# Keeping three windows of the intermediate image in SBUF between two layers, and moving their stores

## The chip, the cores and the metric

The kernel runs on one core of a Trainium2 chip. The metric is the device time of one execution in microseconds (us), the median of several runs; lower is better. TensorE is called PE (its weight loads PEld), VectorE DVE, ScalarE ACT, GpSimd POOL and SyncE SP; SP, ACT and POOL also issue DMAs.

## The reference

Two residual layers on an image x of 48 channels and 256 x 256 pixels, in float32. `_gn` is a group norm over 16 groups of 3 channels.

```python
# layer 0: x = x + L0(gn(x))
qkv = dwconv3x3(einsum('bchw,oc->bohw', x, w_qkv), w_dw)
q, k, v = split(qkv, 3)                 # each cut into 4x4 patches, 8 heads of 96 values
q = l2norm(q); k = l2norm(k)
attn = softmax(einsum('bhcn,bhcm->bhnm', q, k) * temperature)
out = fold(einsum('bhcn,bhnm->bhcm', v, attn))
out = einsum('bchw,oc->bohw', out, w_proj)
# layer 1: x = x + L1(gn(x)), on windows of 64 x 64 pixels
out = einsum('bcphqw,twW,thH,tcC->bCpHqW', xb, Ws, Hs, Cs)      # t runs over 3
```

## The kernel before

Layer 0 begins with the group norm's statistics and the projection to q, k and v, whose results go to DRAM. The attention then runs head by head (`for h in range(NH)`, 8 heads) and in each head over 16 groups of two query blocks. In one group PE computes the scores of two blocks (`logits`, L344), ACT takes their exponential (L563), DVE the reciprocal of the sums and the scaled values vn (L576 to L582), and PE the weighted sums in four parts k (`weigh`, L592), which DVE adds up in `oacc` (L603). All engines stand in the order in which this part is written (`tc.manual_schedule()`). When a head ends, `store(h, m)` for m = 0 to 7 transposes the sums (L609), copies them (ACT, L611, two buffers `oo`) and writes them to the DRAM buffer `os_` through POOL's DMA queue (L613), two DMAs for each m.

The pools of the attention are then closed and the output projection begins, L727 to L755. It has eight tiles t. Tile t holds 16 image rows of the upper half of the image on partitions 0 to 47, and the 16 rows that stand 128 below them on partitions 48 to 95. Of each tile SP loads the attention's result `pot` (from `os_`) and x (`pxt`), 1.5 MB each as two DMAs; PE multiplies by the block matrix `wp`, four times two matmuls of 512 columns (L739); DVE adds the result to x in place, in four additions (L746), and gathers the statistics of the sum in eight `bn_stats` (L750); POOL's queue stores the sum, which is x1, in DRAM as `x1s` (L755). Here the order of each engine's instructions is set by a scheduler, which knows the engines' work and not the other traffic.

The projection's PSUM tiles take the place of the attention's, so that the first L739 waits until ACT's last L611 has read the last transposes.

After the last tile `group_stats` (L135 to L153) makes mean and reciprocal deviation of each group, and a second small matmul (L763) makes the deviation again in the layout of two halves on partitions 0 and 64 (`rstd2`). The matrices Cs are scaled by it (`csn`, L775), and a bias comes from the mean (L779, L781).

Layer 1 works in eight units u: four windows of 64 rows, two halves of 128 columns. Each has three contractions: `over_c` over the channels (PE L834, with x1 as the stationary operand; DVE L841 subtracts the bias into `lzt`), `over_w` (PE L856, ACT copies, L863) and `over_h` (PE L873). `residual` adds the rows of x1 (DVE L885) and sends them out on POOL's queue (L888). Before its use x1 is loaded twice from `x1s`, with different layouts: by channels (`load_x`, L808, three buffers, two units ahead) and by rows (`load_rows`, L817, two buffers for a whole unit). The first `over_c` stands alone; each later one is interleaved with the unit before. In this part too all engines keep the written order. Three lines of it:

```python
parts[u, q].append(over_w(u, c0, c0 + 4))   # for b in 0, 1, each followed by two steps of over_c(u + 1)
over_h(*late)                               # after both b: the third before
late = u, q
```

Of the kernel before, what the change touches and what calls it, by code (L numbers as in the profile page):

```python
# [16 lines left out]
C = 48  # L17
# [3 lines left out]
KS = 4  # L21
# [23 lines left out]
def conv_preact_kernel(  # L45
# [47 lines left out]
    wp = const.tile([P2, P2], F32, name="wp")  # L93
    nc.vector.memset(wp, 0.0)
    for s in range(2):
        r = slice(s * C, (s + 1) * C)
        for h in range(NH if s == 0 else H0):
            o = s * M0 + h * HC if h < H0 else (h - H0) * HC
            nc.scalar.dma_start(
                out=(wq[r] if h < H0 else wr[0:C])[:, o : o + HC].rearrange("c (z e) -> c z e", z=3),  # L100
                in_=w_qkvT.rearrange("c (z h e) -> h c z e", z=3, h=NH)[h],
            )
        nc.scalar.dma_start(out=wp[r, r], in_=w_projT)
# [22 lines left out]
    mean1 = const.tile([P2, 1], F32, name="mean1")  # L126
    rstd1 = const.tile([P2, 1], F32, name="rstd1")
# [7 lines left out]
    def group_stats(st, mean, rstd, pool, pspool):  # L135

        mv = pool.tile([P2, 2], F32, name="mv")
        nc.vector.bn_aggr(mv, st.rearrange("p n s -> p (n s)"))
        pm = pspool.tile([P2, 1], F32, name="pm", tag="pstat")
        nc.tensor.matmul(pm, lhsT=gm, rhs=mv[:, 0:1], start=True, stop=True)  # L140
        nc.vector.tensor_copy(mean, pm)
        d = pool.tile([P2, 1], F32, name="gsd")
        nc.vector.tensor_sub(d, mv[:, 0:1], mean)
        e = pool.tile([P2, 1], F32, name="gse")
        nc.vector.scalar_tensor_tensor(e, d, d, mv[:, 1:2], ALU.mult, ALU.add)
        pv = pspool.tile([P2, 1], F32, name="pv", tag="pstat")
        nc.tensor.matmul(pv, lhsT=gm, rhs=e, start=True, stop=True)
        f = pool.tile([P2, 1], F32, name="gsf")
        nc.vector.tensor_scalar_add(f, pv, EPS)
        g = pool.tile([P2, 1], F32, name="gsg")  # L150
        nc.scalar.activation(g, f, AF.Sqrt)
        nc.vector.reciprocal(rstd, g)
        return mv, e  # L153
# [255 lines left out]
    with tc.tile_pool(name="xn", bufs=1) as xnp, tc.tile_pool(name="cst", bufs=1) as cst, tc.tile_pool(  # L409
# [19 lines left out]
        group_stats(st0, mean0, rstd0, cst, nps)  # L429
# [48 lines left out]
    cv = attention.enter_context(tc.tile_pool(name="cv", bufs=1))  # L478
# [42 lines left out]
    with tc.tile_pool(name="ahead", bufs=2) as ah, tc.tile_pool(name="ae", bufs=3) as ae, tc.tile_pool(  # L521
# [94 lines left out]

        load_query(0, 0)
# [14 lines left out]
        with tc.manual_schedule():  # L632
            load_query(0, 1)
            block = scores(0, 0)
            for h in range(NH):
                more = h + 1 < NH
                rows = {r: Depthwise(h + 1, r) for r in range(CR + 1)} if more else {}
                for g in range(NG):
                    p, d, n = rows.get(g - 2), rows.get(g - 1), rows.get(g)

                    if h == 0 and 0 < g <= 6:
# [40 lines left out]
                    for k in range(NK):  # L682
# [28 lines left out]
                        if g == NG - 1 and k > 0:  # L711
                            for m in range(2 * k - 2, 2 * k):
                                store(h, m)
            for m in range(6, 8):
# [5 lines left out]
    RP = TP // PX * KS  # L720
    NP = TP
    with tc.tile_pool(name="pj", bufs=3) as pj, tc.tile_pool(name="pjs", bufs=1) as pjs, tc.tile_pool(
        name="pps", bufs=3, space=PSUM
    ) as pps, tc.tile_pool(name="pp1", bufs=1, space=PSUM) as pp1:
        st1 = pjs.tile([P2, HALF * W // 512, 6], F32, name="st1")
        ov = os_.rearrange("t (c k) n -> t c k n", k=KK)
        for t in range(HALF // RP):  # L727
            ot = pj.tile([P2, KK, NP], F32, name="pot")
            xt = pj.tile([P2, RP, W], F32, name="pxt")
            for s in range(2):  # L730
                r = slice(s * C, (s + 1) * C)
                y0 = s * HALF + t * RP
                nc.sync.dma_start(out=ot[r], in_=ov[s * (NT // 2 // TP) + t])
                nc.sync.dma_start(out=xt[r], in_=xc[:, y0 : y0 + RP, :])
            xv = xt.rearrange("p (py ki) (px kj) -> p ki kj py px", ki=KS, kj=KS)
            for ki in range(KS):
                ps = pps.tile([P2, KS, NP], F32, name="pps")
                for i in range(0, KS, 2):
                    nc.tensor.matmul(  # L739
                        ps[:, i : i + 2, :],  # L740
                        lhsT=wp,
                        rhs=ot[:, ki * KS + i : ki * KS + i + 2, :],
                        start=True,
                        stop=True,
                    )
                nc.vector.tensor_add(  # L746
                    xv[:, ki], ps.rearrange("p k (py px) -> p k py px", py=RP // KS), xv[:, ki]
                )
            for i in range(0, RP, 2):
                nc.vector.bn_stats(  # L750
                    st1[:, (t * RP + i) // 2, :], xt[:, i : i + 2, :].rearrange("p a b -> p (a b)")
                )
            for s in range(2):
                y0 = s * HALF + t * RP
                nc.gpsimd.dma_start(out=x1s[:, y0 : y0 + RP, :], in_=xt[s * C : (s + 1) * C])  # L755

        gm2 = pjs.tile([P2, 64 + C], F32, name="gm2")
        nc.vector.memset(gm2, 0.0)
        for o in (0, 64):
            nc.vector.tensor_copy(gm2[:, o : o + C], gm[:, 0:C])  # L760
        mv1, e1 = group_stats(st1, mean1, rstd1, pjs, pp1)
        pc1 = pp1.tile([64 + C, 1], F32, name="pc1", tag="pstat")
        nc.tensor.matmul(pc1, lhsT=gm2, rhs=e1, start=True, stop=True)  # L763
        rstd2 = l1c.tile([64 + C, 1], F32, name="rstd2")
        nc.vector.tensor_scalar_add(rstd2, pc1, EPS)
        nc.scalar.activation(rstd2, rstd2, AF.Sqrt)
        nc.vector.reciprocal(rstd2, rstd2)

        csn = l1c.tile([64 + C, T3 * C], F32, name="csn")
        for s in range(2):  # L770
# [4 lines left out]
            nc.vector.tensor_scalar_mul(csn[r], csn[r], rstd2[r])  # L775
# [5 lines left out]
        nc.vector.tensor_copy(cbias, pb1)  # L781


    with tc.tile_pool(name="lx", bufs=3) as lx, tc.tile_pool(name="lz", bufs=2) as lz, tc.tile_pool(
        name="lr", bufs=2
    ) as lr, tc.tile_pool(name="ly", bufs=4) as ly, tc.tile_pool(name="ps1", bufs=2, space=PSUM) as ps1, tc.tile_pool(
# [171 lines left out]
```

## Time and profile before

| | us |
|---|---|
| median of 3 runs | 3771.0 (3754.03 to 3777.11) |
| the profiled execution | 3774.41 |
| its span | 3772.6 |
| last attention matmul (L592) starts its last piece | 3298.4 |
| first projection matmul (L739) | 3318.2 |
| end of the last bn_stats (L750) | 3455.9 |
| csn ready (L775) | 3461.6 |
| layer 1's matmuls run without a stop from | 3475.2 |

PE is busy for 93% of the span, DVE for 58%, ACT for 45%, POOL for 16%; the mean granted clock of PE is 0.97. The times are on the clock of the profiled execution, which starts with its first instruction. A group in a listing has the line, engine and operation, the tiles written and read, partitions x elements, the number of instructions, busy time and mean, and what ended the idle time before it. In a listing by time the columns are the start, the time and the instruction, with the idle time before it in brackets. DMA transfers show in the queues' shares and as what ends a wait.

### The profile page before, as it was taken

To read this page: it belongs to the slowest core of one execution; us is meant where nothing else is said; L and a number is where in the kernel's file an instruction comes from. 1 tells how busy PE (TensorE), PEld (TensorE's weight loads), DVE (VectorE), ACT (ScalarE), POOL (GpSimd) and SP (SyncE) were. 2 spreads that over 40 slices of the span, in tenths; PEclk is the share of its full clock that TensorE was granted. 3 is DMA by queue.
4 is the path that set the end of the run, shared out by engine and by line. 5 is a ranking of instruction groups with operands and counts; after the bars stand their busy time and mean duration, and the time that the engine had idled before them with its cause. 6 is when DMAs were issued, how large, how long until landed. Compare 5 with 4: busy or idle time off the path is not lost.

```text
span 3772.6 us, 100069 instructions
## 1 busy us (share of the span) xinstructions
PE 3521.1 (93%) x44252; PEld 2916.8 (77%) x44252; DVE 2185.9 (58%) x3514; ACT 1715.5 (45%) x2667; POOL 597.5 (16%) x593
## 2 busy tenths in 40 slices
PE   1877999999999999999999999999999999955998
PEld 0335777788888888888888888888888888812776
DVE  5463675169727962896299439934992222256664
ACT  0224565555545554555455445545554444300222
POOL 0031121012301220122122112211221100010011
PEclk9988999999999999999999999999999999966999
DMA  6575666534433542354245424542543100199784
GB/s 144 170 172 159 178 192 177 166 111 118 114 83 99 126 113 73 104 125 107 84 106 122 101 77 113 119 104 75 125 114 93 46 19 23 31 242 199 128 145 91
DMA packets 307826, 441.64 MB, mean 117 GB/s; under 512 B 98474, under 2 KB 232954, under 8 KB 303160
## 3 DMA queue, kind: packets, MB, share of 16 engines
q1 hardware_dynamic: 253668, 269.65, 27.7%
q0 software_dynamic: 48320, 156.61, 18.5%
q10 hardware_dynamic: 5396, 8.88, 1.1%
q8 instruction: 351, 5.75, 0.7%
q14 instruction: 91, 0.75, 0.1%
HBM read 234.76 MB, written 199.95 MB: 115 GB/s over the span
## 4 chain that ended last, share of the span: by engine, by line
PE 84%; DMA 5%; issue 2%; ACT 0%; SPq 0%; DVE 0%; POOL 0%; ACTq 0%; POOLq 0%
PE big L344 37%; PE big L592 36%; PE pb L856 4%; PE pa L834 2%; PE pc L873 2%; PE big L185 2%; DMA x1s<-pxt 1%; DMA pxt<-in_x_dram 1%; DMA t<-ot 1%; PE pt L609 1%; PE pst L546 1%; PE pn L258 1%; DMA kt<-qkv 0%; DMA os__70<-oo 0%; DMA lxq<-x1s 0%
## 5 line engine op out<-in xcount | busy, mean ns | idle before, releaser
L563 ACT ACTIVATE e<-big,nmx 128x1024 f32<-128x1024 f32 x1024 | 1143.9, 1118 | 833.8 <-PE big L344 622.4
L344 PE MATMUL big<-kt,qt 128*128 128x512 f32 x6144 | 1438.9, 393 | 44.4 <-DMA qt<-qkv 31.6
L592 PEld LDWEIGHTS big<-vn,e 128*64 128x64 f32 x32768 | 1365.8, 137 | 83.4 <-ACT e L563 45.1
L592 PE MATMUL big<-vn,e 128*64 128x96 f32 x32768 | 1423.5, 247 | 5.0 <-ACT ot L188 3.1
L344 PEld LDWEIGHTS big<-kt,qt 128*128 128x128 f32 x6144 | 1145.1, 188 | 307.6 <-issue 46.2
L603 DVE TENSOR_TENSOR oacc<-big,oacc 128x768 f32<-128x768 f32 x480 | 458.1, 954 | 708.5 <-PE big L592 708.5
L239 DVE SCALAR_TENSOR_TENSOR acc<-pad,dwt,acc 126x1024 f32<-126x1024 f32 x592 | 766.2, 1295 | 39.1 <-ACT acc L220 23.5
L297 POOL TENSOR_TENSOR ol<-o,oh 126x1024 fp32r<-126x1024 f32 x78 | 187.1, 2399 | 925.3 <-DVE ss L254 800.9
L576 DVE TENSOR_REDUCE zt<-zs 128x1 f32<-128x4 f32 x256 | 38.9, 152 | 360.4 <-ACT e L563 360.4
L563 ACT ACTIVATION_READ_ACCUMULATOR e<-big,nmx 128x1 f32 x1024 | 196.2, 192 | 0.0
L841 DVE TENSOR_TENSOR lzt<-pa,cbias 128x864 f32<-128x864 f32 (+1 forms) x88 | 137.0, 1628 | 96.9 <-PE pa L834 96.9
L863 ACT COPY lyt<-pb 128x512 f32<-128x512 f32 x144 | 84.5, 586 | 212.9 <-PE pb L856 212.9
L302 POOL DMA_DIRECT2D qkv<-o x72 | 88.6, 1230 | 517.6 <-DVE zu L578 248.9
L613 POOL DMA_DIRECT2D os__70<-oo x128 | 65.2, 515 | 599.6 <-ACT oo L611 598.9
L250 ACT ACTIVATE sq<-acc 126x1024 f32<-126x1024 f32 x74 | 78.2, 1057 | 156.3 <-issue 111.1
L284 DVE TENSOR_TENSOR o<-acc,y 126x1024 f32<-126x1024 f32 x74 | 147.6, 1995 | 0.0
L856 PEld LDWEIGHTS pb<-wsb,lzt 128*64 128x64 f32 x2304 | 125.8, 138 | 27.6 <-issue 19.5
L856 PE MATMUL pb<-wsb,lzt 128*64 128x128 f32 x2304 | 141.7, 279 | 1.3 <-issue 1.3
L188 ACT ACTIVATE ot<-big,bias 108x1024 f32<-108x1024 f32 x64 | 71.1, 1112 | 153.7 <-PE big L185 81.4
L739 PE MATMUL pps<-pot,wp 96*96 96x512 f32 x128 | 78.2, 779 | 58.9 <-DMA pot<-os__70 58.9
L220 ACT ACTIVATE acc<-pad,dwt 126x1024 f32<-126x1024 f32 x74 | 84.1, 1137 | 83.0 <-DMA pad<-t 83.0
L318 POOL DMA_DIRECT2D kt<-qkv x44 | 22.9, 527 | 575.8 <-PE big L344 554.5
(116 smaller groups left out, 1904.5 us busy)
## 6 DMA issues: line engine op xcount, KB each, us to landing
pad<-t SPq DMA_DIRECT2D x78, 761.9 KB
qkv<-ol POOLq DMA_DIRECT2D x78, 504.0 KB, 8.9
qkv<-o POOLq DMA_DIRECT2D x72, 504.0 KB, 6.9
qkv<-oh POOLq DMA_DIRECT2D x70, 504.0 KB, 7.4
t<-ot SPq DMA_DIRECT2D x128, 217.7 KB
qt<-qkv SPq DMA_DIRECT2D x176, 96.0 KB
xs<-in_x_dram SPq DMA_DIRECT2D x128, 96.0 KB
os__70<-oo POOLq DMA_DIRECT2D x128, 96.0 KB, 2.1
```

Source lines behind the costliest of these rows:

```text
L220: nc.scalar.mul(self.acc, self.pad[:, 0:KS, 0:W], dwt[:, self.h, 0:1])
L239: nc.vector.scalar_tensor_tensor(self.acc, self.pad[:, dy : dy + KS, dx : dx + W], dwt[:, self.h, tap : tap + 1], self.acc, ALU.mult, ALU.add,
L284: nc.vector.tensor_tensor(self.o.rearrange("p (a b) x -> p a b x", a=KS), self.acc.rearrange("p a (x b) -> p a b x", b=KS), self.y.rearran ...
L297: eng.tensor_sub(self.ol, self.o, self.oh.bitcast(F32))
L302: eng.dma_start(out=qkv[self.h][i].rearrange("j (c k) n -> (j c) k n", k=KK)[:, :, px], in_=self.o if i == 2 else (self.ol if i else self. ...
L344: nc.tensor.matmul(ps[:, i, :], lhsT=qt[:, r, q0 : q0 + 128], rhs=kts[2 * j + i][:, r // 2, :], start=(r == 0), stop=(r == 2),)
L563: nc.scalar.activation(e[:, j * 1024 : (j + 1) * 1024], ps.rearrange("p a b -> p (a b)"), AF.Exp, bias=nmx[:, b : b + 1], accum_out=zs[:, ...
L592: nc.tensor.matmul(ps[p : p + 64, j // 4, j % 4 * HD : (j % 4 + 1) * HD], lhsT=e[:, mb * 128 + p : mb * 128 + p + 64], rhs=vn, start=(i == 0),
L603: nc.vector.tensor_add(oaccs[h, k], ps[:, :, : 4 * HD], oaccs[h, k])
L841: nc.vector.tensor_tensor(zv[:, :, y0 : y0 + n, :], pa[:, :, : n * T3 * C].rearrange("p s (y k) -> p s y k", y=n), cbias.rearrange("p (u v ...
L856: nc.tensor.matmul(pb[s * WS : (s + 1) * WS, i, :], lhsT=zts[u][:, t * C + c + i, :], rhs=wsb[:, t, :], start=True, stop=True,)
L863: nc.scalar.copy(yt[:, t, :], pb.rearrange("p i x -> p (i x)"))
```

## The change

Tiles of x1 stay in SBUF for three of the four windows, and layer 1's channel contraction reads them there. In parts:

1. The projection's tile t is now half t mod 2 of window t // 2: 16 rows of the window's upper 32 rows on partitions 0 to 47, and 16 rows of its lower 32 rows on partitions 64 to 111. These are the layout and the place from which `over_c` reads. `wp` has its two copies at partitions 0 and 64, and each of the old matmuls becomes two, on PE's tile at row and column 0 and on that at row and column 64 (the first has 64 output columns, of which 16 are zero).
2. The partitions 48 to 63 of each window's x tile have to be zero: a memset of partitions 32 to 63 over 8192 elements stands before the loads of x into each, on DVE for window 0 and on POOL for windows 1, 2 and 3.
3. `convolution` is a new pool of its own for the depthwise convolution, so that its memory can be freed before the last head. In the first group of the last head (h = 7, g = 0) the tile of window 0 is zeroed on DVE and loaded by four DMAs on SP. In the last group, after k = 1, the first `pot` (here `pa`) is loaded.
4. SP's instructions in the projection stand in the written order. Window 1's x1 is stored by POOL's queue as before; those of windows 0, 2 and 3 are stored by SP after all loads. 
5. `group_stats` takes its matrix as an argument and works on 112 partitions, so that the second deviation (`pc1`, `rstd2`) is not needed. The matrix `gm2` is loaded by four DMAs instead of two copies on DVE.
6. Layer 1 takes the windows in the order 0, 2, 3, 1. There is no `load_x`. Window 1's x1 is loaded from `x1s` once, in the buffer of window 0, at the start of unit 1. The rows are loaded in thirds of a unit, with three buffers of a third. `over_h` of the third before stands between the two `over_w` of a third, and `lyt` has three buffers instead of four.

```diff
+                    if not more and g == 0:
+                        convolution.close()
+                        xw = ctx.enter_context(tc.tile_pool(name="xw", bufs=1, side="right"))
...
+                        xts[0] = xw.tile([64 + C, 2 * RP, W], F32, name="xwt")
+                        nc.vector.memset(xts[0][32:64], 0.0)
+                        for sub in range(2):
+                            load_input(xts[0], 0, sub)
...
+                        if not more and g == NG - 1 and k == 1:
+                            pots[0] = pa.tile([64 + C, KK, TP], F32, name="pa")
+                            load_output(pots[0], 0)
...
+        NTP = HALF // RP
+        with tc.manual_schedule(engines={mybir.EngineType.SP}):
+            for t in range(NTP):
+                w, sub = divmod(t, 2)
+                if t:
+                    pots[t] = pj.tile([64 + C, KK, TP], F32, name="pot")
+                    load_output(pots[t], t)
+                if w:
+                    if sub == 0:
+                        xts[w] = (pjs if w == 1 else xk).tile([64 + C, 2 * RP, W], F32, name="xk")
+                        nc.gpsimd.memset(xts[w][32:64], 0.0)
+                    load_input(xts[w], w, sub)
...
+                    ps = pps.tile([128, KS, TP], F32, name="pps")
+                    for i in range(0, KS, 2):
+                        for s in range(2):
+                            m = 64 if s == 0 else C
+                            nc.tensor.matmul(
+                                ps[s * 64 : s * 64 + m, i : i + 2, :],
+                                lhsT=wp[s * 64 : s * 64 + C, 0:m],
+                                rhs=pots[t][s * 64 : s * 64 + C, ki * KS + i : ki * KS + i + 2, :],
...
+                if w == 1:
+                    store_x1(w, sub, nc.gpsimd)
+
+            for w in (0, 2, 3):
+                for sub in range(2):
+                    store_x1(w, sub, nc.sync)
+        group_stats(st1, gm2, mean1, rstd1, pjs, pp1)
...
-        units = [(yw, xh) for yw in range(H // WS) for xh in range(2)]
+        units = [(yw, xh) for yw in (0, 2, 3, 1) for xh in range(2)]
...
-            xq = xqs[u]
+            xq = xts[yw]
...
-            for u in range(2):
-                load_x(u)
...
+                if u == 1:
+                    xts[1] = xw.tile([64 + C, HW, W], F32, name="xwt")
+                    for s in range(2):
+                        nc.sync.dma_start(
+                            out=xts[1][s * 64 : s * 64 + C], in_=x1s[:, WS + s * HW : WS + (s + 1) * HW, :]
+                        )
...
                 for q in range(NQ):
+                    load_rows(u, q)
...
-                    if late:
-                        over_h(*late)
+                        if b == 0 and late:
+                            over_h(*late)
```

## The prediction

> **What bounds the kernel now.** The page gives a span of 3772.6 us, the attention to about 3300. I read the busy time by stretches first:
>
> ```profile
> 3340.00:3360.00 20.00, 10.88 (x21) 3.80 (x20) 13.58 (x13) 0.00 (x0) 1.03 (x2) 0.74 1.03 307
> 3400.00:3420.00 20.00, 8.89 (x16) 3.12 (x16) 16.79 (x20) 0.00 (x0) 2.06 (x4) 0.69 1.02 268
> 3456.00:3475.00 19.00, 3.16 (x10) 2.24 (x10) 4.23 (x13) 0.41 (x2) 0.00 (x0) 0.50 0.94 141
> 3495.00:3765.00 270.00, 267.61 (x3776) 202.73 (x3776) 149.40 (x102) 84.45 (x144) 32.05 (x46) 0.99 0.68 120
> ```
>
> After the stretch and its length come PE, PEld, DVE, ACT, POOL, then PE's clock, DMA share and GB/s. The projection has its DMA engines full (1.02) with PE and DVE waiting; from 3495 layer 1 is all PE. The queues in the projection (3335 to 3435), then in the kernel's opening stretch of loads alone (30 to 68): packets, MB, share of 16 engines.
>
> ```profile
> q1 hardware_dynamic: 1451, 17.88, 73.1%
> q0 software_dynamic: 768, 9.44, 27.4%
> ...
> q1 hardware_dynamic: 370, 4.15, 51.9%
> q10 hardware_dynamic: 369, 3.92, 47.4%
> ```
>
> A unit is one tile's load or store, 1.573 MB. In the projection a load takes 73.1 x 1.573 / 17.88 = 6.43 us and a store 27.4 x 1.573 / 9.44 = 4.57: 17.4 a tile, the period seen. Loads alone take 37.7 x 1.573 / 8.07 = 7.35. In order of time, the seams:
>
> ```profile
> 3288.29 5.34 PE L592 MATMUL big<-vn,e 128*64 128x96 f32 x124 [1.87 <-DVE vn L582]
> 3295.11 1.52 POOL L613 DMA_DIRECT2D os__70<-oo  x3 [325.57 <-ACT oo L611]
> 3301.78 2.03 POOL L613 DMA_DIRECT2D os__70<-oo  x4 [4.20 <-ACT oo L611]
> 3317.59 1.02 POOL L613 DMA_DIRECT2D os__70<-oo  x2 [3.02 <-ACT oo L611]
> 3318.17 9.01 PE L739 MATMUL pps<-pot,wp 96*96 96x512 f32 x16 [6.52 <-DMA pot<-os__70]
> 3407.66 7.65 DVE L746 TENSOR_TENSOR pxt<-pps,pxt 96x1024 f32<-96x1024 f32 x4 [3.21 <-DMA pxt<-in_x_dram]
> 3451.02 4.85 DVE L750 BATCH_NORM_STATS2 st<-pxt 96x6 f32<-96x512 f32 x8
> 3461.01 0.61 DVE L775 TENSOR_SCALAR csn<-csn,rstd 48x144 f32<-48x144 f32 x2
> 3475.19 3.21 PE L834 MATMUL pa<-csn,lxq 48*128 48x144 f32 x22 [5.19 <-DMA lxq<-x1s]
> ```
>
> The last head's stores hop through ACT, POOL and a DMA until 3318; eight tiles follow, with 7.65 + 4.85 = 12.5 us of DVE each inside 17.4; statistics end at 3461.6, and layer 1 waits until 3475.2 for the stores and the reload. Two groups price the memsets:
>
> ```profile
> L413 POOL MEMSET zr<- 128x258 f32 x1 | 0.3, 318 | 0.0
> masks.py:197 POOL MEMSET ident<- 128x128 f32 x1 | 0.2, 205 | 0.3 <-POOLq L947 0.3
> ```
>
> (318 - 205) / 130 = 0.87 ns per element of a partition.
>
> **What the Trainium skill says.** DMA: Bandwidth & Descriptors, section on queues, rings and completion order: an engine goes round the queue rows it has work for, packet by packet. The trace agrees: the small L613 stores land in 2.1 us at the median of 128, but in 5.1 to 6.7 us here, beside loads. TensorEngine Tiling (Array Packing), section Tiling Modes: different tiles can run LdWeights and Matmul in parallel. L873 agrees: 24 records of 64x64 tiles in 2.73 us of the chain, 0.114 each, where L739's of the same 512 columns follow every 0.43. TensorE: Matmul & The Clock Gate, Part 1: default is half clock, released by activity. L739's weight loads come every 0.85 us at the start of a burst and every 0.43 after 4 to 7 us.
>
> **The change part by part**, on the old trace's clock.
>
> 1. Last head, first group. DVE zeroes 8192 elements a partition: row L453 (1134 elements, 1003 ns) and L790 (384, 378) give 0.83 ns, 6.9 us, from 2928.0 to 2934.9, before the two normalisations; the weights are first wanted at 2938.2, so those cover it with some 2 us. SP then issues 3.1 MB of x ahead of the query loads for two blocks on: 14.7 us of DMA from 2936.5, query data after that until about 2955 to 2959 with the stores of that time, wanted at 2957.8 (L344). Cost 0 to 4, I take 1.
>
> 2. The memsets on POOL. In the built order those for windows 2 and 3 stand before the last head's stores, and wait for the last vn (3288.24). 2 x 8192 x 0.87 + 2 x 0.1 = 14.5 us (no row is this long; bounds 12 and 18, which move PE's start by as much): stores begin at 3302.9, not 3295.1. The old hops took 22.2 us to ACT's last copy, which the first L739 waits for (PSUM). Four pairs of stores hop one behind the other, since there are two oo buffers. Without neighbours a hop is 0.6 (copy) + 0.3 + 1.0 (two issues) + 2.1 (landing), about 4 us, in all 13.6: PE at 3317. With loads beside every hop it stays at 22.2: 3326. The first hop now finds the DMA queues empty, the later ones meet the early load of pot 0 and those of pots 1 and 2, so I take 20.3 and PE at 3323.5. Early loading gains nothing there: another wait comes last.
>
> 3. Window 1's memset waits for those stores to land (3329) and takes 7.2: its x load, and every load behind it on SP, issues at 3336.5 (3330 to 3338). Tile 2 wants it only at about 3353, as pots 1, 2 and window 0 are there.
>
> 4. The tiles. DVE: first add 5 us after PE's start (3.9 before; the order starts three PSUM tiles before finishing one), then 8 x 12.6 (12.5 and small gaps): 3429. DMA: from 3336.5, 11 load units and 2 store units, at 11 x 6.43 + 2 x 4.57 = 80 or 11 x 7.35 + 2 x 4.57 = 90; if a store adds only what it added to two lone loads before, 17.4 - 14.7 = 2.7, the upper one is 86. I take 83, then 2 to land and 12.5 of DVE on the last tile: 3434 (3425 to 3446). Stores of windows 0, 2, 3 (12 DMAs) stand on SP after all loads. PE has 32 records a tile, in pairs: 6.8 us warm, 13.7 cold, and a burst warms in 4 to 7; covered by DVE, costing at most a us or so.
>
> 5. Statistics. One pair of tiny matmuls with its sum and root goes (-0.75). ACT's table load (1.28 in the trace, at 3317 under the wait) now stands after the wait for the variance: +1.28. From last bn_stats to csn was 5.75, becomes 6.3; with pb 6.9. x1 is in SBUF: L834 starts at 3441, not 3475.2. Of the 12 stores five wait on SP for ACT's Ws/Hs loads (same semaphores), about 3447, then 2.5 units, 16 us; the first row loads follow, landing near 3468, wanted 43 us after the start (L885 at 3518), 3484. Covered by 16.
>
> 6. Layer 1. PE's work is the same: 297.4 us from 3475.2 to the end. The L808 loads go; PE never waited for them after the first. Row loads come in thirds, three buffers: free 8 us before their third begins, wanted 20 after it. Window 1's reload, 14.7 + rows 2.6 + 2, meets a need 19.5 us later; two PSUM buffers cover a small miss. L873 one step earlier in each third: the last no longer waits for DVE's 1.24: -1.3. Sum 296.1 (bounds 294 and 300).
>
> Sum: 3441 + 296.1 + 1 = 3738.1, 34.5 below the span of 3772.6. The profiled execution took 3774.4, 3.4 above the median 3771.0; 3771.0 - 34.5 = 3736.5, say 3737.
>
> **The rivals.**
> - Loads keep the mixed pace (5.8 a unit) and the hops run free: PE at 3317, DVE-bound, 5 + 101: 3423; that is 11 before the forecast's 3434: 3737 - 11 = 3726. For it: the 307 GB/s of the first stretch above. Against: the opening loads at 213 with full engines. 0.20, range 3718 to 3731.
> - A new wait takes the room: the two halves do not pair on PE (13.7 warm a tile, 109 in all), or loads at 7.35 with late rows. Tiles ending at 3447 (13 late) and 4 to 5 of stalls in layer 1: 3754, up to 3770. 0.11.
> - Slower: PE neither pairs nor warms, 32 x 0.853 = 27.3 a tile, 218 for eight; 3323.5 + 218 + 7 for the last add and bn_stats is 3549, 115 behind the forecast: about 3852. For it: PEclk of 0.66 to 0.74 here, and PE waits every tile. Against: L873's packing; a PE so busy has no idle to cool in. Slower by 1% means a span of 3810, so tiles that end at 3810 - 296.1 - 1 - 6.9 = 3506: it decides from (3506 - 3328) / 8 = 22 us a tile. 0.05.
>
> **How the numbers follow.** Forecast 0.64, own range 3729 to 3752. About 1% (37.7 us) is what a measurement here tells from no change: 3733.3. A quarter of the forecast's chance, 0.16, lies below it, with the first rival 0.36 faster; 0.48 + 0.11 = 0.59 within; 0.05 slower. Leaving out 0.05 of the first rival, most of the second and the third, the range is 3724 to 3754.
>
> **What would show it.** POOL memsets of 7.2 us from 3288, twice; PE's first projection matmul near 3323; tile starts 12.5 to 15 apart; a table load between variance and root; L834 (L872 then) starting 7 us after the last bn_stats; 296 from there. Wrong, if POOL's memsets are of another size, tiles take 17 again, or PE shows row waits in layer 1.

## The result, and the profile after

The changed kernel takes 3804.5 us (median of 4 runs, 3797.9 to 3810.3), the kernel before 3771.8 beside it: 1.0086 times the time, with a 95% interval of 1.0064 to 1.0109. So it is slower by 0.9%, where 34 us less were forecast; 3804 lies far above the range of 3724 to 3754. The profiled execution after took 3797.9, with a span of 3796.1.

The two traces by stages, in us, with the forecast on the same marks. Each stage ends where the next begins. "First product of layer 1" is, in the kernel before, the one from which its products run without a stop.

| stage | before | forecast | after |
|---|---|---|---|
| to the end of the last vn (L582, L584 after) | 3288.2 | 3289.2 | 3300.1 |
| to the issue of window 1's first x load | | 48.3 | 61.1 |
| to the end of the last bn_stats | 167.6 from vn | 97.5 | 115.3 |
| to the first product of layer 1 (L834, L872) | 19.3 | 7.0 | 6.7 |
| layer 1 to the end | 297.4 | 296.1 | 312.9 |
| span | 3772.6 | 3738.1 | 3796.1 |

(The forecast's rows come from its 3336.5, 3434 and 3441, with the one us of its step 1 in the first row.) The forecast is 58.0 us short: 10.9 in the last head, 12.8 in the hops, 17.8 with the tiles, 16.8 in layer 1, and -0.3 in the statistics. Only the last-named came out as forecast; the four others are longer. Of the 58.0, 34.5 are the gain that was forecast and did not come, and 23.5 are what the span is longer than before.

Last head, PE in order of time (start, time, instruction; in brackets the idle time before it and what ended it):

```profile
2965.48 2.61 PE L594 MATMUL big<-vn,e 128*64 128x96 f32 x57
2971.93 6.93 PE L594 MATMUL big<-vn,e 128*64 128x96 f32 x128 [3.84 <-issue]
2984.45 0.90 PE L594 MATMUL big<-vn,e 128*64 128x96 f32 x7 [5.59 <-issue]
2985.28 5.00 PE L344 MATMUL big<-kt,qt 128*128 128x512 f32 x14
```

PE stands twice in the middle of a group of equal matmuls, and no semaphore is named: "issue" means that the profile shows nothing that it waited for. The kernel before has no wait of PE at all between 2940 and 3000. PE is also slower after the first stall: 128 matmuls in 6.93 us, where the same number took 5.50 at 2936.7; its clock is 0.83 between 2970 and 2980, and 1.00 before 2970.

The seams behind it, on POOL, ACT and PE:

```profile
3300.19 13.79 POOL L784 MEMSET xk<- 32x8192 f32 x2 [332.10 <-DVE vn L584]
3313.93 2.02 POOL L615 DMA_DIRECT2D os__70<-oo  x4
3351.48 1.01 POOL L615 DMA_DIRECT2D os__70<-oo  x2 [3.80 <-ACT oo L613]
3354.24 6.92 POOL L784 MEMSET xk<- 32x8192 f32 x1 [1.74 <-DMA os__70<-oo]
```

```profile
3335.64 0.58 ACT L613 COPY oo<-pt 96x512 f32<-96x512 f32 x1 [12.57 <-DMA os__70<-oo]
3343.61 0.58 ACT L613 COPY oo<-pt 96x512 f32<-96x512 f32 x1 [7.39 <-DMA os__70<-oo]
```

```profile
3351.29 10.87 PE L793 MATMUL pps<-pa,wp 48*64 48x512 f32 x32 [5.95 <-issue]
```

The two memsets take 13.8 us (14.5 forecast), and the stores begin 13.9 us after the last vn. But from the first pair of stores to the last it takes 37.6 us, since ACT's copy waits up to 12.6 for an old store to land. PE's first product of the projection starts 0.1 us after the end of ACT's last copy (3351.19), which it waits for; "issue" only says that the profile names no releaser.

The tiles on DVE, the DMA queues in two stretches (3365 to 3390, then 3425 to 3450: packets, MB, share of 16 engines), and the busy times of the same two (stretch, length, PE, PEld, DVE, ACT, POOL, PE's clock, DMA share, GB/s):

```profile
3417.25 5.71 DVE L800 TENSOR_TENSOR xk<-pps,xk 112x1024 f32<-112x1024 f32 x3 [5.98 <-DMA xk<-in_x_dram]
3434.24 5.77 DVE L800 TENSOR_TENSOR xk<-pps,xk 112x1024 f32<-112x1024 f32 x3 [4.53 <-DMA xk<-in_x_dram]
```

```profile
q1 hardware_dynamic: 317, 3.88, 102.5%
...
q1 hardware_dynamic: 461, 5.69, 101.0%
```

```profile
3365.00:3390.00 25.00, 21.64 (x62) 6.96 (x62) 23.38 (x23) 0.00 (x0) 0.00 (x0) 0.73 1.02 155
3425.00:3450.00 25.00, 25.00 (x51) 7.64 (x50) 19.22 (x22) 0.00 (x0) 0.00 (x0) 0.51 1.01 227
```

The DMA engines are full, as before, but move 155 GB/s where the kernel before moved 251 to 307. A load unit of 1.573 MB, alone on the queues, takes 1.025 x 25 x 1.573 / 3.88 = 10.4 us in the first stretch and 7.0 in the second. DVE takes 12.5 us a tile, and 14.3 in the two early tiles in which it also waits for PE (up to 1.3 at a time). In tiles 4 and 5, counted from 0, it waits for x: their first additions start 20.3 and 17.0 us after those of the tile before. In the last tile it takes 15.0 us, 2.2 of them waits for PE.

Statistics and layer 1 (ACT and PE in order of time, then PE's waits from 3480 on: us in total, times, longest):

```profile
3480.80 1.28 ACT L152 ACT_TABLE_LOAD   x1 [129.61 <-DVE gsf L151]
```

```profile
3483.20 0.60 PE L872 MATMUL pa<-csn,xwt 48*128 48x144 f32 x1
...
3553.39 2.08 PE L872 MATMUL pa<-csn,xk 48*128 48x144 f32 x14 [3.88 <-issue]
3555.39 4.39 PE L894 MATMUL pb<-wsb,lzt 128*64 128x128 f32 x48
```

```profile
PE pb L894 <- DVE lzt L879: 9.2, 7, 1.3
PE pa L872 <- issue: 3.9, 1, 3.9
```

The statistics went as forecast. In layer 1 PE now waits seven times for DVE's `lzt`, and stands once more with the label "issue", while window 1 is loaded back; the 48 products after it take 4.39 us instead of 2.86 to 2.93.

### The profile page after: what moved, and what is told of

The parts are those of the page before. It is cut to its first block, busy times and chain, and to the rows that moved or that the text cites. A ratio compares the mean times of both kernels' runs of the same rounds, so it can differ in the third digit from the quotient of the medians.

```text
span 3796.1 us, 100386 instructions
## 1 busy us (share of the span) xinstructions
PE 3555.5 (94%) x44378; PEld 2926.7 (77%) x44378; DVE 2192.9 (58%) x3511; ACT 1716.4 (45%) x2666; POOL 611.1 (16%) x584
## 5 line engine op out<-in xcount | busy, mean ns | idle before, releaser
L894 PEld LDWEIGHTS pb<-wsb,lzt 128*64 128x64 f32 x2304 | 127.4, 139 | 38.1 <-issue 31.2
L894 PE MATMUL pb<-wsb,lzt 128*64 128x128 f32 x2304 | 143.1, 281 | 10.6 <-DVE lzt L879 9.2
L254 DVE TENSOR_REDUCE ss<-sq 126x64 f32<-126x1024 f32 x80 | 97.5, 1220 | 23.2 <-ACT sq L250 23.2
```

What stands on the lines that cost most here:

```text
L254: nc.vector.tensor_reduce(self.ss, self.sq.rearrange("p a (x b) -> p x a b", b=KS), AX.XY, ALU.add)
L894: nc.tensor.matmul(pb[s * WS : (s + 1) * WS, i, :], lhsT=zts[u][:, t * C + c + i, :], rhs=wsb[:, t, :], start=True, stop=True,)
```

## The experiments

Each kernel is the changed one with the edit shown, unless it says otherwise; `...` stands for lines left out. What is read is a stage of its trace; the totals of single runs differ for reasons outside the stage (the kernel before took 3766 to 3789 in 28 runs beside one group of these). "The tiles" are the time from the first projection matmul to the last bn_stats. In four kernels whose tile code is equal (the changed one, loads spread, loads behind, layer 1 mended) they took 125.2, 130.7, 128.9 and 131.8 us, so that single runs do not tell apart what differs by less than some 7 us there.

### Last head: spread the loads

```diff
-                        for sub in range(2):
-                            load_input(xts[0], 0, sub)
+                    if not more and 1 <= g <= 4:
+                        sub, s = divmod(g - 1, 2)
+                        nc.sync.dma_start(
+                            out=xts[0][s * 64 : s * 64 + C, sub * RP : (sub + 1) * RP], in_=xc[:, image_rows(0, s, sub), :]
+                        )
```

> The changed kernel, with window 0's four input loads (0.79 MB each) issued one per group at the top of groups 1 to 4 of the last head instead of all four at the top of group 0; the DVE memset stays where it is. Theory A (TensorE's instruction refills stand behind the 3.1 MB backlog of the loads, which made the two stalls of 3.8 and 5.6 us labelled issue): at most three packets per DMA engine stand ahead of a refill, the two stalls fall under 1 us, and the last normalisation of V ends 10 to 13 us earlier than in the changed kernel (near 3288 instead of 3300.1 us on its trace); everything behind keeps its length. Theory C (the memset on DVE, or the new order of the last head, costs the time): the last normalisation stays near 3300.

Measured: from the first exponential of the head to the last vn 354.0 us. It is 354.0 before and 367.3 after. PE has no wait between 2940 and 3000. The memset on DVE is still there, so it costs nothing; the 13.3 us come from the loads' being issued in one piece. The run took 3791.5 us.

### Last head: the block of loads behind the query loads

```diff
-                        for sub in range(2):
-                            load_input(xts[0], 0, sub)
...
                     elif more:
                         load_query(h + 1, g + 2 - NG)
+                    if not more and g == 0:
+                        for sub in range(2):
+                            load_input(xts[0], 0, sub)
```

> The changed kernel, with the four input loads of window 0 issued behind the query loads of the same group on SP, still in one piece. Theory A (instruction refills behind the backlog): the backlog is the same 3.1 MB, so TensorE still stands 7 to 10 us with the label issue in the groups behind it, and the last normalisation of V stays within 3 us of 3300. Theory B (the query loads, queued behind the input loads on SP, come late for the scores): the stalls go, and it ends near 3288 to 3290.

Measured: 361.7 us for the head, last vn at 3298.6, and one stall instead of two:

```profile
2983.53 0.90 PE L594 MATMUL big<-vn,e 128*64 128x96 f32 x7 [6.11 <-issue]
```

So the order on SP is not the cause of 7.7 of the 13.3 us; at most 5.6 belong to it, or to the fact that one packet fewer of the following kind fell into the backlog. What PE waited for shows in the packet records of a queue that the profile calls "instruction" (q8, 16 KB each, called refills here; start, and duration in brackets, us):

```
kernel          refills on q8 between 2940 and 2990                                PE goes on at
before          2941.32  2948.31  2961.71  2969.67  2974.61  2988.91               no stall
after           2946.30  2968.86 (1.63)  2981.63 (1.43)  2985.62                    2971.93, 2984.45
loads behind    2943.83  2951.00  2965.52  2980.41 (1.68)  2989.84                  2983.53
loads spread    2942.43  2948.75  2964.68  2972.30  2975.92                         no stall
```

In each of the three stalls PE goes on 1.4 us after such a packet ends. That these packets carry PE's instructions is read from the counts: from one of them to the next PE runs 128 matmuls at the median (127 in the kernel before), with about as many weight loads; the kernel before has 351 packets for 44,252 matmuls. Up to the late packets PE had run 254 matmuls since the last one in the changed kernel, and 257 with the loads behind, that is two packets' worth, and then it stood; after the first late packet it ran 128 more and stood again. In the changed kernel the two packets start at 2968.86 and 2981.63, and the 3.1 MB of x, issued from 2959.5, have all passed the DMA engines at 2982.2. So the refills of PE's instructions came late while the loads filled the DMA engines; that they stood in line there is the reading that fits both edits.

### Hops: the memsets behind the stores

```diff
-        with tc.manual_schedule(engines={mybir.EngineType.SP}):
+        with tc.manual_schedule(engines={mybir.EngineType.SP, mybir.EngineType.Pool}):
+            for w in (1, 2, 3):
+                xts[w] = (pjs if w == 1 else xk).tile([64 + C, 2 * RP, W], F32, name="xk")
+                nc.gpsimd.memset(xts[w][32:64], 0.0)
             for t in range(NTP):
...
-                    if sub == 0:
-                        xts[w] = (pjs if w == 1 else xk).tile([64 + C, 2 * RP, W], F32, name="xk")
-                        nc.gpsimd.memset(xts[w][32:64], 0.0)
```

> The changed kernel, with the memsets of windows 1, 2 and 3 on POOL put in program order behind the last head's stores, instead of those of windows 2 and 3 ahead of them. If the 13.8 us of the two memsets stand on the path in full: the first store is issued within 1 us of the last normalisation of V's copy chain, the time from the end of the last normalisation to the first projection matmul falls from 51.2 to about 37 us, and the end comes 11 to 14 us earlier (near 3783 on its own span). Rival: the slow landings of the stores (5 to 13 us each beside the loads of the attention output) alone set the chain, the early start only waits longer at the next landing, and it stays above 47 us.

Measured: from the last vn to the first projection matmul 46.2 us instead of 51.2, and the run took 3801.6 us. Neither expectation gave that size. The first store is issued 8.5 us after the last vn, but from the first to the last it is still 37.9 (ACT in order of time):

```profile
3305.80 0.58 ACT L613 COPY oo<-pt 96x512 f32<-96x512 f32 x1 [0.45 <-DMA os__70<-oo]
3322.93 0.58 ACT L613 COPY oo<-pt 96x512 f32<-96x512 f32 x1 [16.56 <-DMA os__70<-oo]
```

The rival's mechanism, the slow landings, is the one that shows. And the 5 us were lost again with the tiles: 139.2 us, 125.2 in the changed kernel.

### Hops: no load beside the stores

With the edit above, and in the loop of the tiles (pot 0 is no longer loaded in the last head, and window 1's input, issued ahead of all pots, waits for the memset behind the stores):

```diff
+            for sub in range(2):
+                load_input(xts[1], 1, sub)
             for t in range(NTP):
-                if t:
-                    pots[t] = pj.tile([64 + C, KK, TP], F32, name="pot")
-                    load_output(pots[t], t)
+                pots[t] = (pj if t else pa).tile([64 + C, KK, TP], F32, name="pot" if t else "pa")
+                load_output(pots[t], t)
...
```

> The changed kernel, with no large load beside the last head's stores: the three memsets of windows 1 to 3 stand on POOL behind the stores, window 1's input loads wait for the first of them, and all loads of the attention output (the one issued in the last head too) stand behind these on SP. Theory (each 2 or 4 KB packet of a store waits for a 16 KB load packet of 1.4 to 1.8 us that its DMA engine runs first): with the queue clear the stores land within 3 us, as the run of small stores in the earlier heads did in 2.1 us, and the time from the first store issued to the last falls from 37.4 us (34 to 38 with or without the memsets ahead) to 17 to 21 us. Rival (the two buffers of oo and the chain of transposes, copies and stores cost that by themselves): it stays above 30 us. The tiles start later, since their loads do: no gain in the end is expected from either.

Measured: 12.3 us from the first store to the last, less than expected (POOL in order of time):

```profile
3309.63 1.52 POOL L615 DMA_DIRECT2D os__70<-oo  x3 [336.67 <-ACT oo L613]
3313.49 2.03 POOL L615 DMA_DIRECT2D os__70<-oo  x4 [1.38 <-ACT oo L613]
3320.86 2.16 POOL L615 DMA_DIRECT2D os__70<-oo  x4 [1.56 <-ACT oo L613]
```

So 25 of the 37.6 us come from the loads beside the stores (with the memsets moved alone it was 37.9). The stores' own packets are short in the records: 0.08 us at the median for 2 KB and 0.23 for 4 KB here, 0.14 and 0.32 beside the loads of the changed kernel. A load packet of 16 KB takes 1.5 us at the median there. That each store packet waits for a load packet is not seen in the records one by one; it is the reading that fits, and it agrees with what the Trainium skill says in DMA: Bandwidth & Descriptors, section on queues, rings and completion order: an engine goes round its rows packet by packet. The kernel before had 2.59 MB of loads between 3295 and 3318 (22.5 us of hops), the changed one 4.72 between 3314 and 3352, since its tiles 0, 1 and 2 read what the first four pairs of stores wrote, where before the lower half of tile 0 waited for the fifth. That the larger amount made the hops longer was not tested by itself.

The projection starts late here, as its loads do, and the run took 3803.9.

### Hops: four buffers of oo

The two further buffers, `late_oo`, come from a small pool that is opened in the last head.

```diff
-            oo = asm.tile([HD, 512], F32, name="oo", bufs=2)
+            other = h == NH - 1 and m % 4 > 1
+            oo = (late_oo[0] if other else asm).tile([HD, 512], F32, name="oo", bufs=2)
```

> The changed kernel, with four buffers instead of two for oo in the last head. If the copies' wait for a buffer makes the chain: from the first store to the last 22 to 25 us instead of 37.4. If the packets of the loads beside the stores make it (18 load packets per DMA engine at 1.5 us stand between them whatever the number of buffers): 30 to 36 us.

Measured: the stores are issued within 19.4 us, better than the first expectation. But the last of them lands only at 3344.9, 33.8 after the first issue; the second expectation had 30 to 36 us, though for the last issue. POOL's memset of window 1 waits for that landing, and with it the x loads.

```profile
3344.95 6.92 POOL L786 MEMSET xk<- 32x8192 f32 x1 [13.37 <-DMA os__70<-oo]
```

PE begins 33.1 us after the last vn, 18 earlier than in the changed kernel, and then waits for x: from the last vn to the last bn_stats it is 173.9, against 176.4. More buffers move the wait from the copies to the landing. The run took 3792.1.

### Tiles: stores beside the loads

```diff
-                if w == 1:
-                    store_x1(w, sub, nc.gpsimd)
...
-            for w in (0, 2, 3):
-                for sub in range(2):
-                    store_x1(w, sub, nc.sync)
+                store_x1(w, sub, nc.gpsimd)
```

> The changed kernel, with every tile's x1 stores issued on POOL as soon as the tile is done, as window 1's are, instead of all six others behind the loads on SP. Theory (the loads alone run at 1.7 us a 16 KB packet, and at 1.0 to 1.2 us where stores run between them, so stores beside loads cost nothing): load packets between the third tile and the last fall from 1.7 to about 1.1 us, and the time from the first projection matmul to the last bn_stats stays at 118 to 130 us (125.2 in the changed kernel). Rival (a store takes its own time on the DMA engines, three packets of 0.8 us on each engine and store, 29 us for twelve): 145 to 160 us.

Measured: 130.5 us for the tiles, at the edge of the first expectation, and 3802.5 for the run. The queues between 3360 and 3370, with loads alone, and between 3375 and 3415, with stores between them:

```profile
q1 hardware_dynamic: 111, 1.56, 103.2%
...
q1 hardware_dynamic: 508, 6.23, 61.3%
q0 software_dynamic: 430, 5.31, 39.1%
```

A load unit takes 1.032 x 10 x 1.573 / 1.56 = 10.4 us alone, and 0.613 x 40 x 1.573 / 6.23 = 6.2 with the stores between; a store 4.6. Two loads and a store are 17.0, two loads alone 20.8. So a tile's loads and store together took less time than its loads alone, and to put the stores behind the loads saved nothing that shows: 130.5 lies among the four kernels with equal tile code. In the packet records the load packets take 1.6 to 1.95 us from 3362 to 3374 and 0.75 to 1.3 after that, where tile 0's stores have begun (medians of stretches of 2 us).

### Tiles: the order of the loads

The added argument takes one of the two halves.

```diff
-                    load_output(pots[t], t)
...
-                    load_input(xts[w], w, sub)
+                    load_output(pots[t], t, (0,))
+                    load_input(xts[w], w, sub, (0,))
+                    load_output(pots[t], t, (1,))
+                    load_input(xts[w], w, sub, (1,))
```

> The changed kernel, with the loads of each tile issued in the order of the kernel before, that is attention output and input for the first half of the image, then both for the second, instead of attention output twice and input twice. If this order makes the kernel before load at 1.0 to 1.2 us a 16 KB packet between its stores: load packets of the tiles 1 to 3 fall from 1.7 to about 1.1 us, and from the first projection matmul to the last bn_stats it takes 105 to 112 us instead of 125.2. If the order has no part in it: still 1.7 us and 120 to 132 us.

Measured: 148.6 us for the tiles and a run of 3829.2, longer than either expectation. Load packets take 1.8 us at the median. The order of before does not make the pace of before; the tiles are longer with it.

### Layer 1: over_h alone, in the kernel before

```diff
                     for b in range(2):
                         c0 = b * 24 + q * 8
                         parts[u, q].append(over_w(u, c0, c0 + 4))
                         for _ in range(2):
                             next(ahead, None)
-                    if late:
-                        over_h(*late)
+                        if b == 0 and late:
+                            over_h(*late)
```

> The kernel before, with one part of the change alone: in layer 1 the products over the height stand between the two products over the width of a step, one step earlier than before. Theory: the last short step of the next unit's channel products loses its cover, so TensorE waits 1.3 us for DVE at each of seven changes of unit (9.2 us in all) while the end gains 1.3: layer 1, from its first channel product to the end, goes from 297.4 to 304 to 306 us. Rival (what layer 1 lost came from the reload of window 1 and the clock after it alone): 296 to 298 us.

Measured: layer 1 takes 3779.5 - 3473.0 = 306.5 us, against 297.4, and the run 3781.3. PE's wait for `lzt` ahead of `over_w` in layer 1:

```profile
PE pb L856 <- DVE lzt L841: 9.2, 7, 1.3
```

They are the same seven waits as in the changed kernel. The kernel before has none of them.

### Layer 1: both causes mended

```diff
                         if b == 0 and late:
                             over_h(*late)
+                        if b == 0 and q == NQ - 1:
+                            next(ahead, None)
...
-                    for s in range(2):
-                        nc.sync.dma_start(
-                            out=xts[1][s * 64 : s * 64 + C], in_=x1s[:, WS + s * HW : WS + (s + 1) * HW, :]
-                        )
...
                     load_rows(u, q)
+                    if u in (1, 2) and q < 2:
+                        s, y = u - 1, q * (HW // 2)
+                        nc.sync.dma_start(
+                            out=xts[1][s * 64 : s * 64 + C, y : y + HW // 2],
+                            in_=x1s[:, WS + s * HW + y : WS + s * HW + y + HW // 2, :],
+                        )
```

> The changed kernel with two edits in layer 1: the last short step of the next unit's channel products is issued one product earlier, behind the products over the height, and window 1 is loaded back in four quarters behind the row loads of four steps instead of in two halves ahead of them. Theory: TensorE's seven waits of 1.3 us for lzt go (9.2 us), the 3.9 us stall labelled issue and the 1.5 us of a cold clock behind it go, and layer 1, from its first channel product to the end, takes 297 to 300 us instead of 312.9. Rival (the waits move to another step, because VectorE has no slack there): 306 to 312.

Measured: layer 1 takes 295.7 us, a little below the expectation, and the run 3786.2. There is no wait for `lzt` in front of L894, and none of PE with the label issue. The reload's stall is of the kind seen in the last head: in the changed kernel an instruction packet runs at 3550.38 for 1.31 us, between load packets of 32 KB and 3.5 to 4.1 us, and PE goes on at 3553.39. It had run 256 matmuls since the packet before, which started at 3529.1. Both edits were made together here. Of the 17.2 us between 312.9 and 295.7, the 9.2 are shown by the run before this one, and 5.4 are the stall and the slow matmuls after it, which are gone with the loading in quarters; some 2.6 are not placed.

### The mended kernel

The changed kernel with the spread loads, four buffers of oo, the memsets behind the stores, the two edits of layer 1, and window 1's tile in memory that is free early (its pool opened ahead of the pots' pool). The last of these was not tried alone.

> The changed kernel with five edits together: window 0's loads spread over four groups; four buffers of oo in the last head; the memsets of windows 1 to 3 behind the stores on POOL, window 1's tile in memory that is free before the stores land; the last short step of the channel products one product earlier; window 1 loaded back in quarters. If the causes found are right and add up: 354 us for the last head, 20 to 24 us from its first store to its last, 155 to 165 us from the last normalisation to the last bn_stats (176.4 in the changed kernel, 167.6 before), 296 us for layer 1: an end near 3750 us, 0.4 to 0.7% faster than the kernel before. Rival (the 84 load packets per DMA engine at 1.7 us, 143 us of them behind the stores, set the tiles whatever stands ahead of them): 172 to 182 us from the last normalisation to the last bn_stats, and an end of 3766 to 3776, no faster than before.

Measured: 3752.4 us (median of 9), 0.9944 times the kernel before, interval 0.9923 to 0.9965: faster than both kernels, and 0.6% faster than the one before. Its stages: 354.0 for the last head, 18.5 from the first store to the last, 162.6 from the last vn to the last bn_stats, 296.4 for layer 1. The first expectation holds in all but the hops, which are 1.5 us below it. Against the changed kernel's trace that is -13.3, -13.8 and -16.5, and -1.6 in the statistics, where the table load came ahead of the wait again. The tiles by themselves have gained nothing: 137.9, where they took 137.7 in the kernel before and 125.2 in the changed one. They start 26.5 us earlier after vn and wait for x on DVE for 2.5 to 8.9 us in each of the last six tiles, two of which are:

```profile
3386.59 5.70 DVE L806 TENSOR_TENSOR xk<-pps,xk 112x1024 f32<-112x1024 f32 x3 [8.93 <-DMA xk<-in_x_dram]
3403.52 5.78 DVE L806 TENSOR_TENSOR xk<-pps,xk 112x1024 f32<-112x1024 f32 x3 [4.45 <-DMA xk<-in_x_dram]
```

Two more were tried on it. The first has the order of the loads of before:

> The same five edits, and the loads of each tile in the order of the kernel before. If the order of the loads matters: 10 to 20 us less than the kernel with the five edits. If not: the same within 4 us.

Measured: 3768.3 us (median of 20; 0.9983, 0.9972 to 0.9994), 16 us more than without this order, which neither expectation had. Its profiled execution has 150.3 us for the tiles: this order is slower in both kernels that have it. The second loads x through ACT's queue, whose written order is kept too:

```diff
         def load_input(xt, w, sub):
             for s in range(2):
-                nc.sync.dma_start(
+                nc.scalar.dma_start(
```

> The kernel with the five edits, with the input loads of windows 1 to 3 issued on ACT instead of SP, so that each DMA engine alternates between two rows of loads, and no input load stands behind one of the attention output that waits for a free buffer. If one row of loads alone is what runs at 1.4 to 1.7 us a packet: load packets near 1.1 us and 110 to 122 us from the first projection matmul to the last bn_stats instead of 137.9. If the loads together are at their pace whatever the row: packets of 1.4 to 1.8 us again and 130 to 145 us.

Measured: 3772.2 us (median of 12; 0.9997, 0.9982 to 1.0013) and 157.1 for the tiles, above both expectations: PE now waits for pots, 27.1 us in all. Two queues of loads are hardly faster together (166 GB/s between 3355 and 3385, from the queues' 4.97 MB).

## Why the prediction was wrong

1. **Last head: cost 1 taken, 13.3 measured** (354.0 to 367.3; 10.9 of it shows in the end times, as the changed trace came 1.4 ahead into this head). The step followed the block of loads to the next data that stood behind it on SP, the queries, and found them covered. What failed is the path: the step left out that PE's instructions come through the same DMA engines. The runs show it: with the block spread the head is back at 354.0. The memset was covered, as the step said, but not where it said: it ran from 2952.6 to 2959.5, behind a store's landing, and not from 2928.0, so that the loads were issued 23 us later than the step has them. No wait for a query shows at that time either, but that was luck: the step had looked at another time.

2. **Hops: 20.3 taken, 37.6 measured from store to store; PE at vn + 35.3 taken, vn + 51.2 measured.** The memsets' time was right: 13.8 for two, 14.5 taken. That it moves PE's start by as much was not: with the memsets moved behind the stores PE starts 5.0 earlier (51.2 to 46.2), as the stores then wait longer for their landings. The hop without neighbours was about right too: 13.6 in all taken, 12.3 with the loads away. The upper bound was wrong. It took the old hops as the worst case, "with loads beside every hop", though the new tile order let three pots load beside them where the old one held the lower half of the first back: 4.72 MB instead of 2.59. That loads beside the stores cost 25 us is shown; that the greater amount is what lengthened the hops is argued from these figures.

3. **Window 1's load: 48.3 after vn taken, 61.1 measured.** The memset, 6.9, was right; the stores' landing, which it waits for, is step 2's error.

4. **Tiles: 83 us of DMA taken for 11 load and 2 store units, 97 measured** (from 3361.2 until the bytes of 11 load units have passed at 3458.1). The other 3.9 of the 17.8 us stand between the loads and the end: DVE begins the last tile 3.4 us after them (2 taken), and needs 15.0 us for it (12.5 taken), with 2.2 of waits for PE. So DVE's price held (12.5 a tile where nothing holds it) and so did PE's pairs (32 matmuls of half size in 10.9 us), but PE, at a clock of 0.50 to 0.74, was not wholly covered. The main term that failed is the load unit: 6.43 from the old mixture of loads and stores, 7.35 from the opening of the kernel, 10.4 and later 7.0 measured. The old mixture was the cheap case. The price per unit was read in it and then used for a stage out of which the change takes most of the stores. Both bounds came from stretches of another kind, and the second was taken for the worst. The prediction's own sign of being wrong, tiles that take 17 again, appears where DVE waits for x.

5. **Statistics: 7.0 taken, 6.7 measured**, with the table load after the wait as said, and x1 not waited for.

6. **Layer 1: 296.1 taken, 312.9 measured.** The step counted what one step earlier gains at the end, and not what `over_h` had covered in the old place: DVE's last `lzt`, for which PE waits 1.3 us, seven times, 9.2 in all; the kernel before with this edit alone has the same waits. (The gain itself, 1.3, is hardly seen: 306.5 in the kernel before with this edit, where 297.4 + 9.2 - 1.3 is 305.3.) The rest is the reload's stall of 3.9 and the slow clock after it, 1.5; some 2 us are not placed. The row loads, which the step looked at, cost one wait of 2.9 on DVE.

None of the rivals was the case. The second, a new wait of some 16 us, had the kind of the event and neither its places nor its size; the slower one, PE that does not pair, did not occur: PE did pair, and what the tiles waited for was mainly x. What made the kernel slower is four misses of 11 to 18 us each, three of them through the DMA engines.

## What to carry to other kernels

A large load that nothing waits for can still delay everything else that the same DMA engines carry: here small stores on the way to a buffer, and PE's own instructions. Issue it in pieces, spaced so that each is done before the next, and look for stalls labelled "issue" in the middle of equal matmuls. A moved instruction is also taken away from where it was: ask which wait it covered there, not only what it does in the new place. And take the price of a transfer from a stretch with the mixture that the changed kernel will have, not from the one that it ends.

## What was not expected of the hardware

- Loads alone, on one queue, run at 145 to 157 GB/s with all 16 DMA engines full, 1.7 to 2.0 us at the median for a packet of 16 KB. This shows in the changed kernel and in every edit of it whose loads start on quiet queues, in the kernel before too (1.9 at the median from 3290 to 3294). It is the same for the attention's result and for x, and for both halves: in the changed kernel each of the first eight DMAs of the tiles has a median of 1.82 to 1.85, if the packets are counted off in the order of issue. With stores between them the engines move 251 to 333 GB/s, and the same load packet takes 0.7 to 1.2. After a stretch with stores the loads alone go on faster than at first, but not at one pace: 1.15 in the changed kernel, 1.25 to 1.4 in the one with layer 1 mended, whose tile code is the same. Neither the order of the loads nor a second queue removed the slow pace, though the kernel's opening moves 213 on two queues. Why it is slow, and what sets the pace afterwards, stays open. One rival was not tried: each of these loads writes 48 partitions only, and a load over more of them may go at another pace.
- PE's instructions come in 16 KB packets, one every 5 to 15 us in the attention and one for some 128 matmuls with their weight loads. Six traces were counted (before, changed, loads spread, loads behind, layer 1 mended, all mended): wherever PE stands in the attention or in layer 1 for 3.4 us or more with the label "issue", it has run 254 to 258 matmuls since the packet before, or 128 since a late one; everywhere else there are at most 215 from one packet to the next. It goes on 1.3 to 1.7 us after the late packet has ended. A backlog of 3.1 MB made PE stand for 3.8 and 5.6 us, and a reload of the same size, in 32 KB packets, for 3.9.
